# Layer 1's tail: weights of the further tiles fetched by SyncE with register addresses in place of GpSimd's indirect DMAs

## The chip, the core and the metric

The kernel runs as one program on one core of a Trainium2 chip. The metric is the time of one execution on the device, in microseconds (us). A core has five instruction streams that are used here, each strictly in order: TensorE (PE, matmuls and transposes), VectorE (DVE), ScalarE (ACT), GpSimd (POOL) and SyncE (SP). SP does no arithmetic in this kernel: it issues DMAs. POOL does element-wise work and also issues the indirect DMAs, whose row numbers come from a table in SBUF.

## What is computed

Two transformer layers on x of shape (8, 256, 128), all in float32. Each layer is adaptive layer norm, causal attention with 16 heads, a gated residual, a second adaptive layer norm and a mixture of experts. Layer 1's mixture, which is what the change touches, is in essence:

```
p        = sigmoid(h @ gate_w + gate_b)            # 16 experts
v, e     = top_k(p, 2);  v = v / sum(v)            # 2 experts for each token
y[e]     = (silu(h @ wg[e]) * (h @ wu[e])) @ wd[e] # hidden size 64
x        = x + gb * (h + shared_mlp(h) + v0 * y[e0] + v1 * y[e1])
```

Which experts a token takes is known only on the device, so the tokens of an expert have to be collected at run time.

## The kernel before

Tokens are held in four groups of 512 (`NW = 4`). For the first three groups of layer 1, the mixture is done sparsely: `route1` picks the experts, and `place_steps` scatters each token's row (indirect DMAs of POOL, line 916) to the DRAM tensor `xs`, which is sorted by expert. The last group, whose routing is known too late, is done densely at the end (`dense_hidden`, `dense_gate`, `dense_project`).

The sorted rows are worked in 40 tiles of 128 rows, four tiles to a step, so ten steps `m = 0..9` (`NQ = 10`). The tiles of steps 0 to 3 are the first 128 rows of each of the 16 experts: their place and their weights are known beforehand, and the weights lie in SBUF already. The tiles of steps 4 to 9, the further tiles, hold whatever is above 128 rows. Which expert each of these tiles has is worked out by `tables_steps` into two tables: `rowi` (first row in `xs`) and `widx` (first row of the expert's weights, plus the partition).

Each step has these parts, by their functions:

- `fetch_rows1(m)` (lines 1717 to 1726) loads the rows into `xg`. For m of 4 and above these are four DMAs of SP with a register as address (line 1026). The registers are filled beforehand, all 24 of them in one go, by `find_rows1` (line 1017, a register load from `rowi`). `xg` has four buffers.
- `fetch_weights1(m)` (lines 1732 to 1745), only for m of 4 and above, loads four times 128x256 floats (128 KB each) into `wt`. For m = 4 and 5 these are a register load from `widx` (line 1741) and a DMA of SP (line 1745) for each tile. For m = 6 to 9 they are an indirect DMA of POOL for each tile (`load_weights`, line 1030).
- `turn1(m)` transposes the rows on PE (line 1760), copies them out of PSUM on ACT (line 1762), and then issues `fetch_rows1(m + 4)`.
- `hidden1(m)` does the two hidden matmuls (line 1771), the SiLU on ACT (line 1776) and the product on DVE (line 1777).
- `project_tiles(m)` does the output matmuls (line 1784), copies them to `ysb` on DVE (line 1790) and stores them to the DRAM tensor `ys` by a DMA of SP (line 1791). `ysb` has three buffers, so the copy of step m waits until the store of step m - 3 has landed.

After the ten steps, `gather1` fetches each token's two results from `ys` by 24 indirect DMAs of POOL (line 1038). Each of them may need any row of `ys`, so the first waits for the last store. Then follow the combination (`combine1`, lines 1893 to 1899), the last group's dense mixture and the output.

The order on each engine is written out by hand (`manual_schedule`): an engine's instructions stand in the order in which the functions are called. The attention loop calls steps that are hung on its iterations by `at_end(n, ...)`; its last iterations, 29 to 31, take the tables, the weights of steps 4 and 5, the rows of steps 0 to 3 and the 24 register loads. After the loop the steps are called one by one with the tail of the attention, in this order around the change: `turn1(0)`, `turn1(1)`, `hidden1(0)`, `turn1(2)`, `hidden1(1)`, `project_tiles(0)`, `turn1(3)`, `hidden1(2)`, `project_tiles(1)`, `tables()` (the second half, 13 instructions of DVE), `turn1(4)`, `hidden1(3)`, and so on, with parts of the norm and the routing of batches 6 and 7 (`norms`, `go6`) between them. `spread_last` (line 1627, matmuls of the last batch's attention denominators) stands between `project_tiles(8)` and `project_tiles(9)`.

SP's DMAs go round eight completion semaphores, and a DMA waits until the one eight before it has landed.

Of the kernel before, what the change touches and what calls it, by code (L numbers as in the profile page):

```python
# [557 lines left out]
def fast_path(ctx: ExitStack, tc: tile.TileContext, i: dict, out: bass.AP, bad: bass.AP):  # L558
# [496 lines left out]
    def ps_ln(shape, name):  # L1055
        return pp.tile(shape, F32, tag="p", name=name)
# [5 lines left out]
    z1 = Sorted(xp, "1", E1, 3 * TT, ND1)  # L1062
# [298 lines left out]
    def at_end(n, *steps):  # L1361
        ends.setdefault(n, []).extend(steps)
# [291 lines left out]
    def norm1(bs):  # L1654


        kept = []
        name = f"{bs[0]}_{bs[1]}"

        def tokens():  # L1660
            ht = tokens1[bs] = lp.tile([P, 2 * bs[1], P], F32, tag="ht", name=f"ht1_{name}")
            nc.gpsimd.tensor_tensor(by_batch(ht), by_batch(kept[0]), rows_of_span(mdb1[:, CB], bs), ALU.mult)
            nc.gpsimd.tensor_tensor(by_batch(ht), by_batch(ht), rows_of_span(mdb1[:, SB], bs), ALU.add)

        def add_h():
            xn, xs = kept[0], span_tokens(bs)
            nc.gpsimd.tensor_tensor(by_batch(xn), by_batch(tokens1[bs]), rows_of_span(mdb1[:, GB], bs), ALU.mult)
            nc.gpsimd.tensor_tensor(xs, xs, xn, ALU.add)

        return [  # L1670
            *layernorm_parts(
                bs[0] // 2, md[1], SB, CB, f"1b{name}", ps_ln, lambda w, xn: kept.append(xn),
                range(2 * (bs[0] % 2), 2 * (bs[0] % 2 + bs[1])),
            ),
            tokens, add_h,
        ]
# [37 lines left out]
    NQ = (E1 + ND1) // 4  # L1714
    starts = []

    def fetch_rows1(m):

        xg = sq["x", m] = lp.tile([P, 4, P], F32, tag="xg", bufs=4, name=f"xg1_{m}")
        if m < E1 // 4:  # L1720
            nc.sync.dma_start(
                out=xg, in_=z1.xs.rearrange("(e r) c -> r e c", r=z1.cap)[0:P, bass.ts(m, 4), :]
            )
        else:
            for t in range(4):
                z1.load_rows(xg[:, t, :], 4 * m + t - E1, starts.pop(0))

    def find_rows1(m):

        starts.extend(z1.row_start(4 * m + t - E1) for t in range(4))  # L1730

    def fetch_weights1(m):

        tag, n = {4: ("wt", 2), 5: ("wt", 2), 9: ("rb", 1)}.get(m, ("v", 3))
        wt = sq["w", m] = lp.tile([P, 4, WD1], F32, tag=tag, bufs=n, name=f"wt1_{m}")
        for t in range(4):
            d = 4 * m + t - E1
            if m > 5:
                z1.load_weights(wt[:, t, :], i["wpk1"], d)
                continue  # L1740
            r = nc.values_load(
                z1.widx[0:1, d : d + 1], engines=[mybir.EngineType.SP], min_val=0, max_val=(E1 - 1) * P,
                skip_runtime_bounds_check_because="an expert's number, 128 times",
            )
            nc.sync.dma_start(out=wt[:, t, :], in_=i["wpk1"][bass.ds(r, P), :])  # L1745

    def weights1(m, t):

        rows = bass.ts(t % 2, I1)
        if m < E1 // 4:  # L1750
            e = 4 * m + t
            return w1["wg1"][:, bass.ts(e, I1)], w1["wu1"][:, bass.ts(e, I1)], w1["wd1"][rows, e // 2, :]
        wt = sq["w", m]
        return wt[:, t, 0:I1], wt[:, t, I1 : 2 * I1], wt[rows, t, 2 * I1 :]

    def turn1(m):
        xT_ps = ps_ln([P, 4, P], f"xT1_{m}")
        xg = sq.pop(("x", m))
        for t in range(4):
            nc.tensor.transpose(xT_ps[:, t, :], xg[:, t, :], ident)  # L1760
        xT = sq["xT", m] = lp.tile([P, 4, P], F32, tag="xT", name=f"xTs1_{m}")
        nc.scalar.copy(xT, xT_ps)
        if m + 4 < NQ:
            fetch_rows1(m + 4)

    def hidden1(m):
        xT = sq.pop(("xT", m))
        gu = pp.tile([P, 2, 2, P], F32, tag="s", name=f"gu1_{m}")
        for what in range(2):
            for t in range(4):  # L1770
                nc.tensor.matmul(  # L1771
                    out=gu[bass.ts(t % 2, I1), what, t // 2, :], lhsT=weights1(m, t)[what],
                    rhs=xT[:, t, :], start=True, stop=True,
                )
        a = sq["a", m] = lp.tile([P, 2, P], F32, tag="aq", name=f"aq1_{m}")
        nc.scalar.activation(a, gu[:, 0], AF.Silu)
        nc.vector.tensor_tensor(a, a, gu[:, 1], ALU.mult)

    def project_tiles(m):
        a = sq.pop(("a", m))  # L1780
        y = [pp.tile([P, 2, P], F32, tag=tag, bufs=1, name=f"yq1_{m}_{tag}") for tag in ("o", "sum")]
        for t in range(4):
            k = t % 2
            nc.tensor.matmul(
                out=y[k][:, t // 2, :], lhsT=a[bass.ts(k, I1), t // 2, :], rhs=weights1(m, t)[2],
                start=True, stop=True,
            )
        ysb = lp.tile([P, 2, 2, P], F32, tag="ysb", bufs=3, name=f"ysb1_{m}")
        for k in range(2):
            nc.vector.tensor_copy(ysb[:, :, k, :], y[k])  # L1790
        nc.sync.dma_start(
            out=z1.ys[bass.ds(4 * m * P, 4 * P), :].rearrange("(t p) c -> p t c", p=P),
            in_=ysb.rearrange("p a k c -> p (a k) c"),
        )
# [157 lines left out]
    for bs in ((0, 2), (2, 2), (4, 1), (5, 1)):  # L1952
# [14 lines left out]
        if bs[0] < 5:  # L1967
            at_end(n + 7, add)
    tables = one(z1.tables_steps(ps_ln, True))
    at_end(29, tables, lambda: fetch_weights1(4), lambda: fetch_weights1(5))  # L1970
    at_end(30, *[lambda m=m: fetch_rows1(m) for m in range(4)], *[lambda m=m: find_rows1(m) for m in range(4, NQ)])

    for n in range(N):
        b, u = divmod(n, 4)
# [18 lines left out]
            step()  # L1993


    for m in (6, 7):
        fetch_weights1(m)
    norms = [norm1((b, 1)) for b in (B - 2, B - 1)]
    go6, go7 = (one(route1((b, 1))) for b in (B - 2, B - 1))
    values1(*divmod(N - 1, 4))  # L2000
# [1 line left out]
    turn1(0)  # L2002
    turn1(1)
    hidden1(0)
    for m in (8, 9):
        fetch_weights1(m)
    add()
    turn1(2)
    hidden1(1)
    project_tiles(0)  # L2010
    turn1(3)
    hidden1(2)
    project_tiles(1)
    tables()
# [77 lines left out]
def adaln_two_layers(tc: tile.TileContext, i: dict, out: bass.AP):  # L2092
    nc = tc.nc
    with tc.tile_pool(name="flag", bufs=1) as fp:
        bad = fp.tile([1, 1], mybir.dt.int32, name="bad")
        fast_path(tc, i, out, bad)
        redo = nc.values_load(bad[0:1, 0:1], min_val=0, max_val=1, skip_runtime_bounds_check_because="a comparison")
        with tc.If(redo > 0):
            general_path(tc, i, out)
# [84 lines left out]
```

## Time and profile before

| | us |
|---|---|
| median of 14 runs | 640.78 |
| lowest and highest of them | 635.79, 642.7 |
| the profiled execution, its own time | 643.87 |
| the profiled execution, span from first to last instruction | 641.7 |

Busy shares of the span: PE 88%, PE's weight loads 63%, DVE 54%, POOL 48%, ACT 45%. The attention of layer 1 ends at 542.4 us; the ten steps run from 544.9 to 585.7, the 24 gathers from 589.0 to 619.0, and the rest to 641.7.

An instruction's line such as "570.15 0.66 PE L1760 MATMUL xT<-ident,xg ... x4" is: start in us from the span's start, length in us of the merged group, engine, line of the kernel, operation, output<-inputs, and how many were merged. Brackets at its end give the idle time of the engine before it and what ended it. "SPq" is SP's instruction stream. Register loads and the arithmetic of registers are not counted as busy, so gaps between SP's DMAs may be full of them.

### The profile page before, as it was taken

What the parts mean: (1) busy time and instruction counts of PE and PEld (TensorE: products, weight loads), DVE (VectorE), ACT (ScalarE), POOL (GpSimd) and SP (SyncE); (2) the same over time, 40 slices, a digit from 0 to 9 for tenths busy, and PEclk for the clock granted to TensorE, in tenths of its full rate; (3) what the DMA queues carried; (4) which work ended last, traced back from release to release, by engine and by line L of the source; (5) the groups of instructions that cost most, each with busy time, mean ns of one, the idle gap of its engine ahead of it and who ended that gap; (6) DMA issues with size and microseconds to landing.
All of it is one profiled execution on the core that took longest, in us unless ns stands there. A gap on an engine that the chain in (4) does not pass through costs nothing.

```text
span 641.7 us, 12934 instructions
## 1 busy us (share of the span) xinstructions
PE 565.6 (88%) x4903; PEld 402.0 (63%) x4903; DVE 349.6 (54%) x1055; ACT 289.1 (45%) x502; POOL 307.6 (48%) x454
## 2 busy tenths in 40 slices
PE   4789887988869999869999999999999997887973
PEld 3445444445569999756667676766777765665453
DVE  4225758577663222233844566575746566456586
ACT  2567665555505555426553444335435351452230
POOL 6232557576631444136652234761364737712773
PEclk9979998888989999989999999999999999789787
DMA  8999970012033999513030303130203034742441
GB/s 285 343 408 397 389 259 21 13 56 91 26 115 90 323 324 320 185 49 137 26 84 10 67 10 76 38 80 1 67 17 84 19 68 138 220 134 74 110 100 70
DMA packets 51377, 85.45 MB, mean 133 GB/s; under 512 B 6428, under 2 KB 30108, under 8 KB 50156
## 3 DMA queue, kind: packets, MB, share of 16 engines
q1 hardware_dynamic: 42140, 57.67, 28.2%
q0 software_dynamic: 9168, 26.88, 13.7%
q8 instruction: 40, 0.66, 0.4%
q14 instruction: 29, 0.24, 0.1%
HBM read 53.46 MB, written 31.07 MB: 132 GB/s over the span
## 4 chain that ended last, share of the span: by engine, by line
PE 38%; DVE 6%; POOL 4%; issue 3%; ACT 2%; DMA 2%; SPq 1%; POOLq 0%; DVEq 0%; ACTq 0%
PE sc L1564 7%; PE o L1586 6%; PE qp L1533 5%; PE vp L1546 5%; PE kp L1533 4%; POOL yg L1038 4%; PE y L1639 4%; PE sum L1594 3%; PE gu L1771 1%; PE xT L1760 1%; DMA xg<-xs 1%; DVE tc L1894 1%; SPq L1745 1%; PE rp L1627 1%; ACT L751 1%
## 5 line engine op out<-in xcount | busy, mean ns | idle before, releaser
L804 POOL TENSOR_SCALAR_AFFINE_SELECT pt<-pt 128x256 f32<-128x256 f32 (+1 forms) x176 | 89.0, 530 | 136.7 <-ACT pt L1567 80.2
L1038 POOL DMA_INDIRECT yg<-ys,yidx x56 | 53.8, 960 | 54.5 <-issue 34.0
L1030 POOL DMA_INDIRECT wt<-in_wpk_dram,widx x47 | 44.3, 942 | 56.2 <-PE xT L1312 49.9
L1134 ACT ACTIVATE pt<-sc 128x1024 f32<-128x1024 f32 x48 | 46.6, 1021 | 29.8 <-PE sc L1130 25.9
L1567 ACT ACTIVATE pt<-sc 128x768 f32<-128x768 f32 x64 | 48.4, 808 | 25.5 <-PE sc L1564 25.4
L1323 ACT ACTIVATE hst<-hp,wt 128x128 f32<-128x128 f32 x136 | 38.9, 368 | 31.7 <-ACT hst L1323 18.3
L1564 PEld LDWEIGHTS sc<-q,k 64*128 64x128 f32 x512 | 41.5, 187 | 16.4 <-issue 11.4
L1564 PE MATMUL sc<-q,k 64*128 64x256 f32 (+1 forms) x512 | 50.5, 336 | 0.0
L1586 PE MATMUL o<-pt,v 128*64 128x256 f32 (+1 forms) x512 | 48.7, 332 | 1.8 <-POOL pt L804 1.8
L1549 ACT COPY v<-vp 128x512 f32<-128x512 f32 x32 | 18.8, 586 | 67.7 <-PE vp L1546 56.8
L1333 DVE COPY ysb<-yt 128x128 f32<-128x128 f32 x39 | 11.4, 292 | 61.0 <-PE yt L1329 61.0
L1586 PEld LDWEIGHTS o<-pt,v 128*64 128x64 f32 x512 | 31.8, 136 | 19.7 <-POOL pt L804 5.6
L1537 DVE COPY q<-qp 128x512 f32<-128x512 f32 x32 | 22.0, 688 | 38.9 <-PE qp L1533 38.9
L1321 PE MATMUL hp<-xTs,wt 128*128 128x128 f32 x272 | 36.8, 278 | 3.8 <-DMA wt<-in_wpk_dram,widx 2.7
L1533 PE MATMUL qp<-h,wq 128*128 128x256 f32 x128 | 37.0, 412 | 1.3 <-DVE sh L1282 1.3
L916 POOL DMA_INDIRECT xs<-ht0b,idx x32 | 31.5, 983 | 13.0 <-issue 4.6
L1546 PE MATMUL vp<-wv,h 128*128 128x512 f32 x64 | 36.2, 648 | 1.1 <-DVE q L1537 1.1
L1130 PE MATMUL sc<-qm,k 32*128 32x512 f32 x192 | 34.9, 743 | 2.6 <-ACT pt L1134 1.8
L1321 PEld LDWEIGHTS hp<-xTs,wt 128*128 128x128 f32 x272 | 33.0, 191 | 5.9 <-issue 4.4
L1329 PE MATMUL yt<-wt,hst 128*128 128x128 f32 x272 | 35.8, 275 | 0.0
L1533 PE MATMUL kp<-h,wk 128*128 128x256 f32 x128 | 33.8, 388 | 0.0
L1329 PEld LDWEIGHTS yt<-wt,hst 128*128 128x128 f32 x272 | 33.0, 192 | 0.0
(292 smaller groups left out, 1169.0 us busy)
## 6 DMA issues: line engine op xcount, KB each, us to landing
xs<-zero SPq DMA_DIRECT2D x1, 12288.0 KB
xs<-zero SPq DMA_DIRECT2D x1, 8192.0 KB
rb<-rd SPq DMA_DIRECT2D x14, 512.0 KB
mdb<-mrd SPq DMA_DIRECT2D x2, 2048.0 KB
xg<-xs SPq DMA_DIRECT2D x63, 64.0 KB
wst<-in_wpk_dram SPq DMA_DIRECT2D x5, 514.0 KB
ys<-ysb SPq DMA_DIRECT2D x10, 256.0 KB
ys<-ysb SPq DMA_DIRECT2D x39, 64.0 KB
```

Source lines behind the costliest of these rows:

```text
L804: nc.gpsimd.affine_select(out=pt, in_=pt, compare_op=ALU.is_ge, fill=0.0, base=0, pattern=[[0, pt.shape[1]], [1, P]], channel_multiplier=-1,)
L1030: nc.gpsimd.indirect_dma_start(out=wt, out_offset=None, in_=packed, in_offset=bass.IndirectOffsetOnAxis(ap=self.widx[:, d : d + 1], axis=0),)
L1038: nc.gpsimd.indirect_dma_start(out=yg[:, k, :], out_offset=None, in_=self.ys[:, :], in_offset=bass.IndirectOffsetOnAxis(ap=self.yidx[:, j, ...
L1134: nc.scalar.activation(pt[:, bass.ts(half, 2), :], sc, AF.Exp)
L1321: nc.tensor.matmul(out=hp[:, c, :], lhsT=wt[:, bass.ts(c, P)], rhs=xT, start=True, stop=True)
L1323: nc.scalar.activation(hs[:, c, :], hp[:, c, :], AF.Gelu_apprx_tanh, bias=wt[:, WB + c : WB + c + 1])
L1329: nc.tensor.matmul(out=y, lhsT=hs[:, c, :], rhs=wt[:, bass.ds(WF + c * P, P)], start=(c == 0), stop=(c == FC - 1))
L1533: nc.tensor.matmul(out=ps_[:, n, :], lhsT=w1[f"w{what}1"][:, bass.ts(2 * u + n, P)], rhs=hb, start=True, stop=True)
L1546: nc.tensor.matmul(out=vp, lhsT=hb[:, bass.ts(j, P)], rhs=w1["wv1"][:, bass.ts(half, 512)], start=True, stop=True)
L1564: nc.tensor.matmul(out=sc[:, n, cols], lhsT=k[r, m, bass.ts(kb, P)], rhs=q[r, m, qs], start=True, stop=True)
L1567: nc.scalar.activation(pt, sc[:, :, 0:384], AF.Exp, scale=1.0 / math.sqrt(D1))
L1586: nc.tensor.matmul(out=o[bass.ts(n, D1), m, qs], lhsT=v[:, kb, bass.ts(4 * (u % 2) + 2 * m + n, D1)], rhs=pts[m][:, n, cols], start=(kb == ...
```

## The change

The branch to `load_weights` goes: `fetch_weights1` uses SP's register load and register-addressed DMA for all of steps 4 to 9. The calls for steps 6 to 9 move as well. Step 6's is hung on iteration 30 of the attention loop, behind the 24 register loads; step 7's comes after `hidden1(0)`, step 8's after `turn1(2)`, step 9's after `turn1(3)`. On the other engines nothing is added, removed or put in another order but that POOL's 16 indirect DMAs are gone.

```diff
@@ -1735,9 +1735,6 @@
         wt = sq["w", m] = lp.tile([P, 4, WD1], F32, tag=tag, bufs=n, name=f"wt1_{m}")
         for t in range(4):
             d = 4 * m + t - E1
-            if m > 5:
-                z1.load_weights(wt[:, t, :], i["wpk1"], d)
-                continue
             r = nc.values_load(
                 z1.widx[0:1, d : d + 1], engines=[mybir.EngineType.SP], min_val=0, max_val=(E1 - 1) * P,
                 skip_runtime_bounds_check_because="an expert's number, 128 times",
@@ -1968,7 +1965,8 @@
-    at_end(30, *[lambda m=m: fetch_rows1(m) for m in range(4)], *[lambda m=m: find_rows1(m) for m in range(4, NQ)])
+    at_end(30, *[lambda m=m: fetch_rows1(m) for m in range(4)], *[lambda m=m: find_rows1(m) for m in range(4, NQ)],
+           lambda: fetch_weights1(6))
@@ -1993,8 +1991,6 @@
-    for m in (6, 7):
-        fetch_weights1(m)
     norms = [norm1((b, 1)) for b in (B - 2, B - 1)]
@@ -2002,13 +1998,14 @@
     turn1(0)
     turn1(1)
     hidden1(0)
-    for m in (8, 9):
-        fetch_weights1(m)
+    fetch_weights1(7)
     add()
     turn1(2)
+    fetch_weights1(8)
     hidden1(1)
     project_tiles(0)
     turn1(3)
+    fetch_weights1(9)
     hidden1(2)
     project_tiles(1)
     tables()
```

In SP's stream the order from the 24 register loads on becomes: weights 6, rows 4, rows 5, weights 7, rows 6, weights 8, store 0, rows 7, weights 9, store 1, rows 8, store 2, rows 9, stores 3 to 9. Before, it was the same without the weights, and with rows 6 ahead of store 0 as now.

## The prediction

> **What bounds the kernel now.** I read the chain of waits first, over the tail; then the timelines of SP, PE and POOL from 530 to 592 us, the instructions by line for the fetches, and the busy time by stretch for the clock. The chain shows what the tail hangs on:
>
> ```profile
> 570.90 0.59 ACT xTs L1762
> 571.51 1.28 ACT L1691
> 579.43 3.88 PE rp L1627 x16
> 585.66 2.28 DMA ys<-ysb
> 588.95 0.97 POOL yg L1038
> ```
>
> From 588.95 POOL issues 24 gathers, one each 1.25 us, then four element-wise instructions, and the end follows. All of it stands behind the last `ys` store, issued at 585.66. So what delays step 9's store delays the end one for one, and what only makes POOL idle sooner gains nothing. POOL's timeline says the same of the fetches that go away:
>
> ```profile
> 557.59 0.95 POOL L1030 DMA_INDIRECT wt<-in_wpk_dram,widx  x1 [0.30 <-issue]
> 568.27 0.73 POOL L1668 TENSOR_TENSOR x<-x,xn1b 128x256 f32<-128x256 f32 x1
> 588.95 0.97 POOL L1038 DMA_INDIRECT yg<-ys,yidx  x1 [19.94 <-issue]
> ```
>
> The last weight fetch is issued at 557.59, and POOL then stands idle for 19.94 us before the gathers. POOL is free there. SP is not:
>
> ```profile
> 533.99 7.28 SPq L1745 DMA_DIRECT2D wt<-in_wpk_dram  x8
> 541.36 2.05 SPq L1721 DMA_DIRECT2D xg<-xs  x4
> 551.12 6.21 SPq L1026 DMA_DIRECT2D xg<-xs  x12
> 557.43 0.38 SPq L1791 DMA_DIRECT2D ys<-ysb  x1
> 558.06 2.62 SPq L1026 DMA_DIRECT2D xg<-xs  x4
> 560.79 0.42 SPq L1791 DMA_DIRECT2D ys<-ysb  x1
> 561.46 1.90 SPq L1026 DMA_DIRECT2D xg<-xs  x4
> 563.47 0.39 SPq L1791 DMA_DIRECT2D ys<-ysb  x1
> 564.42 1.93 SPq L1026 DMA_DIRECT2D xg<-xs  x4
> ```
>
> The gap between 543.4 and 551.1 is not idle; by the instructions of line 1017 it is the register loads, end to end:
>
> ```profile
> L1017 SPq TENSOR_LOAD <-rowi x24: 261/267/281, 543.5 to 550.6; - x24
> ```
>
> So SP works without a pause from 533.5 to 557.8, and its rows are late already: rows 4 could go at 545.6, when `turn1(0)` has freed the buffer, and go at 551.12. What saves the steps is that PE consumes slower still. The reader should set the last rows beside the transposes that need them:
>
> ```profile
> 570.15 0.66 PE L1760 MATMUL xT<-ident,xg 128*128 128x128 f32 x4
> 572.76 0.66 PE L1760 MATMUL xT<-ident,xg 128*128 128x128 f32 x4
> ```
>
> These are `turn1(8)` and `turn1(9)`. The last DMA of rows 8 is issued at 563.02 and lands at 564.95, of rows 9 at 566.01 and 567.87 (the trace's landings). The slack is 5.2 and 4.9 us. That is all that SP may be delayed.
>
> **What the change removes.** 16 indirect DMAs of POOL, 16 x 1.25 = 20 us of POOL between 538.8 and 558.6. Behind them stand only the two instructions of `add` (L1667, L1668 at 558.56) and the token instructions at 564.25, which waited 3.94 us for DVE. Nobody waits for either, so this is worth 0 on the path; the cover is POOL's idle 19.94 us. A second effect is on the transfers: POOL's 16 x 128 KB fly at the same time as rows 0 to 3, of which DMA 1 takes 4.84 us to land in the chain of waits and the last one 5.9, while the first took 3.5. `turn1(1)` waited 1.24 us for it. If it landed in 2.28, as a store of the same 256 KB does, it would be there at 544.1, and `turn1(1)` could follow `turn1(0)` at 544.5 in place of 546.8: a gain of up to 2.3 us at the head of the steps. I take 0, because SP's stream behind 543.4 does not wait for PE, and SP is what will be late.
>
> **What it adds to SP.** A weight fetch is a register load, register arithmetic and a DMA. The eight of steps 4 and 5 show the price: their DMAs start at 535.19, 536.05, 536.88, 537.72, 538.55, 539.38, 540.20, so 0.83 us each. A row DMA, whose register is ready, takes 0.53 (551.12 to 557.43 for 12). A store takes about 0.5 with its wait. From the end of the register loads at 550.9, and with no wait on PE in between (steps 0 to 3 are transposed by 554), the stream is:
>
> - weights 6 (4 x 0.83 = 3.3) to 554.2, rows 4 (2.1) to 556.4, rows 5 to 558.5
> - weights 7 to 561.8, rows 6 to 564.0, weights 8 to 567.3, store 0 to 567.8, rows 7 to 570.0
> - weights 9 to 573.3, store 1 to 573.8, rows 8 to 576.0, store 2 to 576.5, rows 9 to 578.6
>
> All 16 weight fetches are queued ahead of rows 8: 13.3 us, of which waits that SP had before (it stood for stores at 557.8, 560.5 and 563.4) give back about 0.8. The last DMA of rows 8 starts at 575.5, of rows 9 at 578.1. Alone, a row DMA lands in 1.8 to 2.2 us (551.12 to 552.93; 566.01 to 567.87); I take 2.1. So rows 8 are there at 577.6 and rows 9 at 580.2, against transposes at 570.15 and 572.76: **+7.45 us each**.
>
> A second line is late by as much. `ysb` has three buffers, so DVE's copy of step 5 waits for store 2. Stores take 2.28 to land; store 2 goes at 576.1 and lands at 578.4, where the copy stood at 570.38: +8.0. Behind it on DVE stands the router's add (L1690 at 571.20, then 579.2), but ACT can use that only after its table load, which follows the copy of `turn1(8)` by 0.6 us and takes 1.28: 577.6 + 0.7 + 0.6 + 1.3 = 580.2, against 572.80. So ACT stays at +7.45, and store 2 has about 0.6 us to spare there.
>
> From there the chain is the old one: SiLU tables, steps 7 to 9, `rp`, store 9 (from 570.15 to 585.66, 15.5 us), then the gathers. Nothing in it is hidden, so +7.45 goes to the end. The weights are in time: weights 9 land near 575, `hidden1(9)` comes after 582.
>
> **PE's clock.** Waiting costs PE its clock. The busy time by stretch shows it after the idle times that end at 544.9 and 562.8:
>
> ```profile
> 546.00:553.00 7.00, 6.20 (x44) 4.91 (x46) 0.42 (x1) 3.23 (x6) 5.17 (x7) 0.51 0.70 202
> 563.00:567.00 4.00, 4.00 (x29) 3.24 (x29) 1.72 (x7) 1.52 (x2) 1.45 (x2) 0.57 0.66 173
> 567.00:572.00 5.00, 5.00 (x62) 4.17 (x62) 2.82 (x8) 2.78 (x6) 1.46 (x2) 1.00 0.42 119
> ```
>
> The seventh column is the granted clock. At half clock a hidden step takes 1.9 us (550.84) in place of 1.02 (568.55). In the changed kernel PE waits for rows 4 from about 555 to 558, and for stores 0 and 1 near 568 to 570.5 and 573.5 to 576.5, so half clock is likely up to about 580 to 583. Up to there SP is later than PE, and it costs nothing. On the path it slows `turn1(8)` (+0.4) and perhaps `hidden1(8)`, half hidden by ACT: +0.5 in all. Bounds: 0 if the clock is full by 577, and +3.9 if it is still half during `rp` (3.88 at full clock).
>
> **A rule against the trace.** The register load is 0.267 us in the row above. The Trainium skill (DMA: Bandwidth & Descriptors, "Latency and other measured facts") gives a floor of about 600 ns for it; by that a fetch would take 0.33 more, 16 of them 5.3, and the forecast would be about 654. The row is of the same instruction on the same engine and decides. The same page ("Issuing engines are not separate DMA queues") says that spreading DMAs over several engines saves only issue time on the sequencers, usually small beside the transfer. Here that issue time is the whole matter, and the change puts it all on one sequencer.
>
> **Sum.** 7.45 + 0.5 = +8.0 us. The profiled execution would have a span of 649.7 and, with the 2.2 around it, a time of 651.9; its own time of 643.87 lies 3.1 above the median. From the median, 640.8 + 8.0 = **648.8 us**. What a measurement of this kernel can tell from no change is about 0.3%, 1.9 us.
>
> **The rivals.**
>
> *SP still worse.* Two of the 32 register-addressed DMAs held SP for 1.06 us in place of 0.33 (540.20, 558.59), both while transfers landed slowly, in over 3.5 us. Were four of the 36 weight and row DMAs up to rows 8 held so, +2.9; with `rp` at half clock, +3.9 in place of 0.5. Together 7.45 + 2.9 + 3.9 = +14, or 655; one of them alone 651.7 to 652.2. For it: the bytes in flight do not fall, they only come by another queue. Against: the first five fetches of steps 4 and 5, before POOL's began, landed in 2.0 to 2.1 us.
>
> *SP less late.* If a fetch's register load ran beside the DMA issue ahead of it, a fetch would cost 0.83 - 0.27 = 0.56, 16 of them 4.3 less, and rows 8 would be late by 7.45 - 4.3 = 3.1 us: 644.4 with the clock's 0.5. Against: seven fetches in a row show 0.83.
>
> *Faster, by the transfers.* Rows 0 to 3 land sooner without POOL's traffic, and the steps start 2.3 us earlier, all of it kept: 640.8 - 2.3 = 638.5. This decides only if SP is not late, that is if a fetch adds under 5.2 / 16 = 0.33 us to SP's stream. The rows of line 1745 say 0.83.
>
> *No effect.* If the weights moved but SP had idle room that I misread, the end stays. The end-to-end register loads speak against it.
>
> **How the numbers follow.** Chances: the forecast (+6.5 to +9.5) 0.68, worse SP (+9.5 to +14) 0.15, less late (+2.5 to +6.5) 0.10, faster 0.05, no effect 0.02. So faster 0.05, same 0.02, slower 0.93. The range leaves out the two sides beyond +3.7 and +12.7: 644.5 to 653.5.
>
> **What would show it.** Right: SP's timeline without a gap from 550.9 to about 578, weight DMAs 0.83 apart; rows 9 issued near 578 instead of 566; PE idle before L1760 with the releaser "DMA xg<-xs" in the later steps and DVE's L1790 idle on stores; the first gather near 597; POOL's gathers still 1.25 apart. Wrong: `turn1(8)` waiting for DVE or ACT and not for rows; weight DMAs much closer or further apart than 0.83; a shift of the first gather that does not reach the end.

## The result, and the profile after

The changed kernel takes 649.17 us (median of 10 runs, 646.72 to 652.23), the kernel before 640.70 (47 runs). The ratio is 1.0147, with a 95% interval of 1.0123 to 1.0172: **slower by 7.9 to 11.0 us**, in the middle 9.4 (the two medians lie 8.5 apart). Forecast were 648.8 and +8.0.

One thing has to be known to read the numbers below. The result and the last experiment ran on chips where the kernel before takes 641 us; the other experiments ran on three chips where it takes 670 to 672. In the experiments each ratio is against runs of the kernel before on the same chip; the kernel before was profiled only where it takes 641. The distance from the first row DMA of step 0 to the last store of `ys` hardly depends on the chip for a kernel in which POOL issues no DMA in that stretch (54.6 us in the changed kernel on the one, 54.2 on the other), so it is used to compare SP's work.

SP's timeline of the changed kernel (L1742 weights, L1026 rows, L1788 stores):

```profile
546.15 2.87 SPq L1742 DMA_DIRECT2D wt<-in_wpk_dram  x4
549.27 4.02 SPq L1026 DMA_DIRECT2D xg<-xs  x8
553.87 3.77 SPq L1742 DMA_DIRECT2D wt<-in_wpk_dram  x4
557.89 1.93 SPq L1026 DMA_DIRECT2D xg<-xs  x4
560.72 2.84 SPq L1742 DMA_DIRECT2D wt<-in_wpk_dram  x4
563.66 0.38 SPq L1788 DMA_DIRECT2D ys<-ysb  x1
564.29 1.89 SPq L1026 DMA_DIRECT2D xg<-xs  x4
566.68 2.83 SPq L1742 DMA_DIRECT2D wt<-in_wpk_dram  x4
569.61 0.38 SPq L1788 DMA_DIRECT2D ys<-ysb  x1
570.23 1.89 SPq L1026 DMA_DIRECT2D xg<-xs  x4
572.23 0.38 SPq L1788 DMA_DIRECT2D ys<-ysb  x1
572.85 1.89 SPq L1026 DMA_DIRECT2D xg<-xs  x4
```

Four weight fetches stand ahead of rows 4, 6, 7 and 8 each. Store 0 goes at 563.66, though DVE had its tile ready at 546.2: it stood in the stream behind them. The chain of waits of the same kernel then runs through a store and not through a row load:

```profile
566.68 0.33 SPq L1742
568.34 0.33 SPq L1742
569.61 2.62 DMA ys<-ysb
572.32 0.44 DVE ysb L1787
572.80 0.58 PE yq_o L1781
574.35 1.04 PE xT L1757 x4
...
590.65 2.27 DMA ys<-ysb
593.13 0.74 issue
593.86 1.00 POOL yg L1038
```

Read upwards from 574.35, which is `turn1(8)`: PE was held by the output matmuls of step 5 (L1781), these by DVE's copy of step 4 (L1787), that by store 1, and store 1 by the weights of step 9. PE, DVE and POOL say what they waited for, in the brackets of their timelines:

```profile
551.24 1.39 PE L1757 MATMUL xT<-ident,xg 128*128 128x128 f32 x3 [3.65 <-DMA xg<-xs]
...
566.38 0.42 DVE L1787 COPY ysb<-yq_o 128x256 f32<-128x256 f32 x1 [5.29 <-DMA ys<-ysb]
...
572.32 0.43 DVE L1787 COPY ysb<-yq_o 128x256 f32<-128x256 f32 x1 [4.34 <-DMA ys<-ysb]
...
593.86 1.00 POOL L1038 DMA_INDIRECT yg<-ys,yidx  x1 [29.08 <-DMA ys<-ysb]
```

POOL now idles 29.08 us ahead of the gathers, where it idled 19.94. Distances from the first row DMA of step 0 (541.36 before, 536.06 after), in us:

| | before | after | difference |
|---|---|---|---|
| `turn1(1)` | 5.43 | 4.01 | -1.42 |
| last DMA of rows 8 | 21.65 | 35.73 | +14.08 |
| `turn1(8)` | 28.79 | 38.22 | +9.43 |
| last store | 44.30 | 54.60 | +10.30 |
| end of the span | 100.35 | 110.94 | +10.59 |

The two profiled executions differ by only 643.87 to 649.15 = 5.28, because the part ahead of the first row DMA, nearly the same code in both, was 5.30 shorter in the second. That part differs as much between profiles of one kernel (541.56 and 537.57 in the two of the constant addresses below), so the tail alone shows the change.

### The profile page after: what moved, and what is told of

The parts are those of the page before. It is cut to its first block, busy times and chain, and to the rows that moved or that the text cites. A ratio compares the mean times of both kernels' runs of the same rounds, so it can differ in the third digit from the quotient of the medians.

```text
span 647.0 us, 12977 instructions
## 1 busy us (share of the span) xinstructions
PE 566.6 (88%) x4903; PEld 405.9 (63%) x4903; DVE 350.0 (54%) x1055; ACT 289.0 (45%) x502; POOL 291.9 (45%) x438
## 4 chain that ended last, share of the span: by engine, by line
PE 38%; DVE 5%; SPq 4%; POOL 4%; issue 3%; DMA 1%; ACT 1%; POOLq 0%; DVEq 0%; ACTq 0%
PE sc L1564 7%; PE o L1586 6%; PE qp L1533 5%; PE vp L1546 5%; PE kp L1533 4%; POOL yg L1038 4%; PE y L1639 4%; PE sum L1594 3%; SPq L1742 1%; PE gu L1768 1%; SPq L1017 1%; SPq L1738 1%; DMA ys<-ysb 1%; DVE tc L1891 1%; SPq L1026 1%
## 5 line engine op out<-in xcount | busy, mean ns | idle before, releaser
L1030 POOL DMA_INDIRECT wt<-in_wpk_dram,widx x31 | 29.1, 939 | 51.3 <-PE xT L1312 49.7
L1321 PE MATMUL hp<-xTs,wt 128*128 128x128 f32 x272 | 36.6, 278 | 2.0 <-DMA wt<-in_wpk_dram,widx 0.8
L1130 PE MATMUL sc<-qm,k 32*128 32x512 f32 x192 | 33.1, 710 | 3.6 <-ACT pt L1134 2.8
```

The source lines that it names most:

```text
L1130: nc.tensor.matmul(out=sc[:, n, :].rearrange("p (a q) -> p a q", q=rhs.shape[2]), lhsT=k[r, cols], rhs=rhs, start=True, stop=True,)
L1321: nc.tensor.matmul(out=hp[:, c, :], lhsT=wt[:, bass.ts(c, P)], rhs=xT, start=True, stop=True)
```

## The experiments

Theory A: the loss is SP's time for issuing 16 more fetches ahead of the rows and stores. Rival B: the loss is the bytes, now in flight at another time or by another queue.

### The issue time without the bytes

The kernel before, with POOL's fetches kept, and on SP at the places of the change 16 register loads and DMAs of 256 bytes:

```diff
+    junk = lp.tile([1, 16, I1], F32, bufs=1, name="junk")
+    def spend1(m):
+        for t in range(4):
+            d = 4 * m + t - E1
+            r = nc.values_load(z1.widx[0:1, d : d + 1], engines=[mybir.EngineType.SP], ...
+            nc.sync.dma_start(out=junk[:, 4 * (m - 6) + t, :], in_=i["wpk1"][bass.ds(r, 1), 0:I1])
```

> The kernel before, with POOL still fetching all weights of steps 6 to 9, and with 16 register loads and register-addressed DMAs of SP added at the places in SP's stream where the changed kernel has its fetches, but each DMA moves 256 bytes into a spare buffer. Theory A (SP's issue time is what costs): if such a DMA costs SP the same 0.83 us, the tail is as late as in the changed kernel, +8 to +10 us, 649 to 651; if a DMA of one row is cheaper to issue, 16 times the measured cost, less the slack of 5 us and the 0.8 of old waits: at 0.55 us a fetch +3, 644. Rival B (the bytes on SP's queue, that is the transfers, cost): within 1 us of before, since no bytes to speak of are added. Shown by the distance of the new DMAs in SP's timeline and by the start of the ninth transpose (turn1(8)) against the fetch of rows 0.

Measured: 679.95 against 671.74, ratio 1.0132 (1.0089 to 1.0176), +8.9 us. In SP's timeline of this kernel, four such fetches of 256 bytes (L1738) take 3.23:

```profile
566.43 3.23 SPq L1738 DMA_DIRECT2D junk<-in_wpk_dram  x4
569.91 3.02 SPq L1026 DMA_DIRECT2D xg<-xs  x4
573.98 3.40 SPq L1738 DMA_DIRECT2D junk<-in_wpk_dram  x4
577.47 0.40 SPq L1803 DMA_DIRECT2D ys<-ysb  x1
```

The fetches start 0.99 us apart, no closer than the 128 KB fetches of the changed kernel (0.82 to 0.87). The issue of the DMA itself takes 0.28 in place of 0.33; the register load ahead of it (L1734) takes mostly 0.48 here in place of 0.27, which was not explained. The chain of waits has the same links as in the changed kernel, from the fetches through store 1 and DVE's copy to `turn1(8)`:

```profile
583.10 0.49 SPq L1734
584.13 2.44 DMA ys<-ysb
586.66 0.43 DVE ysb L1802
587.14 0.58 PE yq_o L1796
588.69 1.04 PE xT L1772 x4
```

The same kernel on a second such chip:

> The kernel of e1 again, with the same theories: A says that 16 loads and DMAs of 256 bytes delay the rows by what they take of SP (0.83 us each if the issue does not depend on the size: +8 to +10 us where the kernel before takes about 641; at 0.55 each +3); B says within 1 us of before.

Measured: 677.60 against 670.98, ratio 1.0106 (1.006 to 1.0152), +7.1 us, the fetches again 1.0 apart. What follows: nearly no bytes, and a loss of the size of the change's 9.4 (6.0 to 11.8 and 4.0 to 10.2 by the intervals). A stands. As a size it is rough, since a fetch is dearer here and SP was slowed at the head on this kind of chip, as shown further down. B is not needed; it isn't excluded that bytes add something.

### A shorter fetch: constant addresses

The changed kernel with the 16 fetches at addresses that are known beforehand, so without register load and arithmetic (these steps then multiply with the weights of other experts):

```diff
+            if m > 5:
+                nc.sync.dma_start(out=wt[:, t, :], in_=i["wpk1"][bass.ts(d % E1, P), :])
+                continue
```

> The changed kernel, with the 16 fetches of steps 6 to 9 at constant addresses: no register load and no register arithmetic, the same bytes by the same queue at the same places. (It computes with the wrong experts' weights.) Theory A: a fetch costs SP about 0.38 us (the issue of 0.33 and a gap), 16 of them 6.1, less 0.8 and the slack of 5: +0 to +1.5 us, 640.7 to 642.2. Rival B (bytes): as slow as the changed kernel, 649 to 650.

Measured: 663.76 against 671.74, ratio 0.988 (0.9852 to 0.9908). On a second chip:

> The kernel of e2 again: the same bytes by SP's queue as in the changed kernel, at constant addresses. A says +0 to +3 us against a kernel before of about 641 (its trace of the first job had the last store 47.0 us behind the fetch of rows 0, against 44.3 before and 54.6 changed); B says as slow as the changed kernel in the same job.

Measured: 660.93 against 670.98, ratio 0.9858 (0.981 to 0.9906). SP's timeline of the first of the two:

```profile
562.27 1.80 SPq L1739 DMA_DIRECT2D wt<-in_wpk_dram  x4
564.17 0.38 SPq L1791 DMA_DIRECT2D ys<-ysb  x1
564.79 1.91 SPq L1026 DMA_DIRECT2D xg<-xs  x4
566.75 1.84 SPq L1739 DMA_DIRECT2D wt<-in_wpk_dram  x4
```

A fetch takes 0.47 here (562.27 to 564.17 for four) in place of 0.83, and the same bytes go by the same queue. 16 x 0.36 = 5.8 less is what A asks for. The last store lies 47.04 and 48.49 behind the first row DMA, against 54.15 in the changed kernel on such a chip: 7.1 and 5.7 less. A sizes it, B gives 0. Of the 5.7, 3.6 are in the medians of the same chip (660.93 against the 664.57 of the next section).

### The changed kernel on a second kind of chip

That these kernels beat 671 was odd, as they are still some 3 to 4 us later at the last store than the kernel before in its profile. So the changed kernel itself was run there:

> The changed kernel itself, beside the experiments, since in the job of the first four the kernel before took 671.7 us, 31 more than in the job of the prediction's result. Theory A: where the kernel before takes about 641, this takes 8 to 11 more. Where the kernel before takes about 672, its tail is held up by something that the first job does not show, in stretches in which all engines crawl; e2 to e4, which take fetches from POOL, were faster than before there by 5 to 13 us, so this could be within 5 us of before on either side.

Measured: 664.57 against 670.98, ratio 0.9882 (0.9844 to 0.992): **faster by 5.4 to 10.5 us there** (the medians are 6.4 apart), with the same lateness at the last store (54.15). Something else costs the kernel before more on such a chip. Fewer and more fetches by POOL show where. Step 6 alone by SP, then steps 6 and 7, then none and those of steps 4 and 5 by POOL as well:

```diff
-            if m > 5:
+            if m not in (4, 5, 6):        # the second kernel: (4, 5, 6, 7); the third: ()
                 z1.load_weights(wt[:, t, :], i["wpk1"], d)
                 continue
```

> Only step 6's weights by SP, at the changed kernel's place; steps 7 to 9 by POOL as before. Theory A: SP is later by 3.3 us, under the slack of 5.2 of rows 8: no change, 639.7 to 641.7, and rows 8 land before their transpose. Rival C (each fetch costs the end its share): a quarter of the loss, +2.4 us, 643.1.

> Steps 6 and 7 by SP, steps 8 and 9 by POOL. Theory A: SP later by 6.7 us, less 0.6 of old waits and the slack of 5.2: about +1 us, 641 to 643. Rival C: half of the loss, +4.7 us, 645.4.

> The opposite of the change: the weights of steps 4 and 5 too by POOL's indirect DMAs, behind the attention's last mask. SP then has no weight fetch at all, and rows 0 to 3 go out when the last scatter has landed (2.8 us sooner than before: 538.6 in place of 541.4). Theory A (SP's stream sets the start of the steps): 2 to 3 us faster than before. Rival D (the steps are set by PE and DVE, and SP's fetches at their head are hidden as well): no change, within 1 us. Rival B (the bytes beside rows 0 to 3): slower, since now all of POOL's fetches fly beside them, +1 to +3.

Measured, with POOL's fetches in brackets: 666.36 (12), ratio 0.9915 (0.989 to 0.994); 658.98 (8), ratio 0.9815 (0.9791 to 0.9839); 683.02 (24) against 670.98, ratio 1.0153 (1.0108 to 1.0198). None of the three is what A had said, no change, about +1 and 2 to 3 less: those sums were for a chip of 641. What orders the four times, with the kernel before, is how many fetches POOL issues: 683, 671, 666 and 659 us at 24, 16, 12 and 8, so 5 to 7 us for each four (with none, in the changed kernel, SP's lateness outweighs the gain). The timelines of the kernel with 12, POOL's last fetches first, then DVE, then ACT:

```profile
550.29 0.95 POOL L1030 DMA_INDIRECT wt<-in_wpk_dram,widx  x1 [0.30 <-issue]
551.54 0.94 POOL L1030 DMA_INDIRECT wt<-in_wpk_dram,widx  x1 [0.30 <-issue]
552.50 0.73 POOL L1667 TENSOR_TENSOR xn1b<-ht,mdb 128x256 f32<-128x256 f32 x1
```

```profile
542.07 0.69 DVE L1598 COPY ou<-o 128x512 f32<-128x512 f32 x1 [2.09 <-PE sum L1594]
554.95 1.76 DVE L1602 RECIPROCAL r<-sum 128x256 f32<-128x256 f32 x1 [12.19 <-remote]
```

```profile
555.00 1.07 ACT L1762 COPY xTs<-xT 128x512 f32<-128x512 f32 x2 [22.78 <-remote]
```

POOL issues its train at 1.25 each and is not slowed. DVE starts nothing from 542.8 to 554.95, 2.5 us after the train's end, though by PE's timeline the matmuls ahead of its reciprocal ended at 541.3. ACT copies the transposes of `turn1(0)` at 555.00, which PE had done at 545.1; the kernel before in its profile (on the other kind of chip) makes that copy at 545.60, in the middle of POOL's train. ACT's idle time ahead of it is 22.78 us here, 26.95 with 24 fetches by POOL and 12.32 in that profile. The releaser "remote" or "issue" names nothing on this core. PE did its two transposes meanwhile and then waited 9.28 for ACT. SP is slowed too: its 24 register loads end 14.56 us behind the first row DMA, in place of 9.5. So on these chips DVE, ACT and SP are held while POOL issues indirect DMAs back to back; by what, these runs do not show. It happens again in the 24 gathers: from the first gather to the end the changed kernel takes 71.6 us there and 53.1 on the other.

### No fetches at all

The changed kernel with the fetches of steps 6 to 9 left out (these steps multiply with weights of other experts, which lie in SBUF):

```diff
-        if m < E1 // 4:
-            e = 4 * m + t
+        if m < E1 // 4 or m > 5:
+            e = (4 * m + t) % E1
-           lambda: fetch_weights1(6))
...
-    fetch_weights1(7)
...
-    fetch_weights1(8)
...
-    fetch_weights1(9)
```

> The changed kernel with the weight fetches of steps 6 to 9 left out: neither POOL nor SP fetches them, and these steps multiply with weights that lie in SBUF already (so their results are of the wrong experts). SP's stream is that of the kernel before, POOL has nothing to issue before the gathers. Theory A (SP's issue time is the whole loss of the changed kernel, and POOL's fetches are worth nothing on the path): the last store lies 42 to 44.5 us behind the first row DMA of step 0, as in the kernel before (44.3) or up to 2.3 less, against 54 to 55 in the changed kernel. Rival B (the weights' bytes, by whatever queue, hold the rows): clearly under 42. Where the kernel before takes about 671 us, this one takes 10 to 15 us less if the hold of the other engines comes from POOL issuing indirect DMAs back to back, and 0 to 3 less if it does not; where it takes 641 us, 0 to 2.5 less.

Measured: 654.09 against 670.38, ratio 0.9742 (0.9694 to 0.9789), by the medians 16.3 less. The last store lies 41.57 behind the first row DMA: 12.6 less than with SP's fetches, and 2.7 less than in the kernel before. A's lower end (42) was missed by 0.4, on the side that rival B had named. The 2.7 is the head's gain that the prediction bounded at 2.3: `turn1(2)` comes at +5.56 in place of +8.36, and with SP on time it is kept to the end. That it comes from the transfers beside rows 0 to 3 was not tested by itself. From the first gather on it still takes 69.0 us, by ACT's timeline with long stops between its instructions:

```profile
588.63 1.28 ACT L1691 ACT_TABLE_LOAD   x1
595.56 0.23 ACT L1691 ACTIVATE p<-p 128x32 f32<-128x32 f32 x1 [5.64 <-issue]
...
619.34 1.09 ACT L1827 ACTIVATE a<-gud 128x512 f32<-128x512 f32 x2 [12.83 <-remote]
```

POOL issues the 24 gathers from 585.45 to 615.2; the instruction at 619.34 had stood 12.83 us and comes only after them. With 16 us for this, the numbers of such a chip add up: without fetches 640.7 - 2.7 + 16 = 654.0 (measured 654.1), changed 649.2 + 16 = 665.2 (664.6). The kernel before is 640.7 + 16 + 14 = 671 if POOL's train of 16 weights costs 14; that last figure is only what is left over.

### The weights by ACT, and later on SP

Two attempts to keep the fetches away from POOL and from the rows. Weights 4, 5, 6 by ACT behind the attention loop, 7 by SP after `turn1(3)`, 8 and 9 after `turn1(5)`:

```diff
+            act = m in (4, 5, 6)
-            nc.sync.dma_start(out=wt[:, t, :], in_=i["wpk1"][bass.ds(r, P), :])
+            (nc.scalar if act else nc.sync).dma_start(out=wt[:, t, :], in_=i["wpk1"][bass.ds(r, P), :])
```

> No weight fetch by POOL, and SP's share made small: weights of steps 4, 5, 6 are fetched by ACT (register load and DMA on ACT, right behind the attention loop, where ACT is idle), those of step 7 by SP after turn1(3), those of 8 and 9 by SP after turn1(5), behind the rows of step 9. Theory A (SP's issue time ahead of the rows is the loss): 4 of the 16 fetches of the changed kernel stay ahead of rows 8 (4 x 0.83 = 3.3 us, within the slack of 5.2), the 8 of steps 4 and 5 no longer stand ahead of rows 0; the last store lies 43 to 47 us behind the first row DMA of step 0, that DMA goes up to 3 us sooner, and the kernel takes 0 to 3 us less than the kernel before where that takes 641, and 12 to 16 less where it takes 671. Rival B (the bytes in flight): the same bytes in the same stretch, so 50 us or more and no gain over the changed kernel.

Measured: 663.50 against 670.38, ratio 0.9901 (0.9874 to 0.9928), so 4.8 to 8.4 less and not A's 12 to 16; the last store at +51.46, not 43 to 47. B's number came out (50 or more, and next to no gain over the changed kernel's 664.57); its cause is looked at below. The other left all 16 on SP, weights 6 after `turn1(3)`, 7 after `turn1(4)`, 8 and 9 after `turn1(5)`:

> The changed kernel with the same 16 fetches on SP, only placed later: weights 6 after turn1(3), 7 after turn1(4), 8 and 9 after turn1(5), so that 8 of them stand ahead of rows 9 and none ahead of rows 7, and the last 8 behind all rows. Theory A: rows 8 are late by 4 x 0.83 = 3.3 us, within their slack of 5.2, rows 9 by 6.6 against 4.9, but stores 1 and 2 and the last weights are pushed too; the last store lies 46 to 50 us behind the first row DMA of step 0, against 54 to 55 in the changed kernel. Rival B (the bytes of the weights, not SP's stream): 53 to 55, since the same bytes come by the same queue. Where the kernel before takes about 671 us: 8 to 11 less than it by A, about 6 less by B; where it takes 641: 2 to 6 more by A.

Measured: 669.66 against 670.38, ratio 0.9997 (0.9968 to 1.0025); the last store at +53.95, where A had said 46 to 50. In time both were off: A had 8 to 11 less, B about 6 less. (Its median lies 5 us above the changed kernel's on another such chip, at the same distance to the last store; the profiled execution, 666.43, is the shortest of ten. That difference is not explained.) B had the distance again, but not the cause: `turn1(8)` comes at +27.63, earlier than in the kernel before, with the same bytes on the same queue. SP's and DVE's timelines of this kernel show what I had left out:

```profile
568.48 1.93 SPq L1026 DMA_DIRECT2D xg<-xs  x4
570.98 6.24 SPq L1742 DMA_DIRECT2D wt<-in_wpk_dram  x8
577.32 15.12 SPq L1788 DMA_DIRECT2D ys<-ysb  x7
```

```profile
579.99 0.42 DVE L1787 COPY ysb<-yq_o 128x256 f32<-128x256 f32 x1 [6.04 <-DMA ys<-ysb]
```

The eight fetches behind rows 9 are ahead of store 3, which goes at 577.32 (+39.2, in the kernel before +25.1). DVE's copy of step 6 waits 6.04 for it. The rows up to 8 were freed and the stores held. In the kernel with ACT it is the same eight and the same store (573.82, +36.6), and one more thing at the head:

```profile
532.62 14.98 ACTq L1744 DMA_DIRECT2D wt<-in_wpk_dram  x12
547.64 1.07 ACT L1761 COPY xTs<-xT 128x512 f32<-128x512 f32 x2 [15.93 <-DMA wt<-in_wpk_dram]
```

ACT needed 15 us for its 12 fetches (0.86 apart, with a stop before the fifth, which by the chain of waits goes at 541.22, when SP's first row DMA has landed; the two share a completion semaphore), and its copy of `turn1(0)`, which could go at 541.9, went at 547.64.

### The same fetch on POOL

The kernel before, with POOL's 16 indirect DMAs replaced by register loads and register-addressed DMAs of POOL, at the same places:

```diff
-            if m > 5:
-                z1.load_weights(wt[:, t, :], i["wpk1"], d)
-                continue
+            pool = m > 5
-                z1.widx[0:1, d : d + 1], engines=[mybir.EngineType.SP], min_val=0, max_val=(E1 - 1) * P,
+                z1.widx[0:1, d : d + 1], engines=[mybir.EngineType.Pool if pool else mybir.EngineType.SP],
-            nc.sync.dma_start(out=wt[:, t, :], in_=i["wpk1"][bass.ds(r, P), :])
+            (nc.gpsimd if pool else nc.sync).dma_start(out=wt[:, t, :], in_=i["wpk1"][bass.ds(r, P), :])
```

> The kernel before with one edit: POOL still fetches the weights of steps 6 to 9, at the same places, but each by a register load of POOL and a DMA with a register address in place of the indirect DMA. SP's stream stays that of the kernel before. Theory A (the loss of the changed kernel is SP's issue time, so the fetches may stay with POOL in any form): the last store lies 41 to 45 us behind the first row DMA of step 0, against 44.3 before and 54 to 55 in the changed kernel. Where the kernel before takes about 671 us there is a second question, what holds the other engines while POOL issues: if it is the indirect form, this kernel takes 10 to 16 us less (as the one without fetches, 16 less); if it is POOL's issuing of DMAs or the bytes, within 3 us of the kernel before. Where the kernel before takes 641: 0 to 3 less. Rival B (the bytes in flight on any queue delay the rows): no better than the kernel before in the distance to the last store.

Measured: 639.61 against 641.32, ratio 0.9983 (0.9957 to 1.0009), on a chip like that of the result. The last store lies at +44.43, against +44.30 before and +54.60 with the change. POOL's timeline:

```profile
545.83 0.54 POOL L1744 DMA_DIRECT2D wt<-in_wpk_dram  x1 [0.81 <-DMA xg<-xs]
546.76 0.54 POOL L1744 DMA_DIRECT2D wt<-in_wpk_dram  x1 [0.40 <-issue]
```

A register-addressed fetch takes POOL 0.93 (the first five 0.53 to 0.61), an indirect one 1.25, and the last goes 10.2 us behind the first row DMA in place of 16.2. Nobody waited for POOL, so the time is the same. This is the cleanest of the comparisons: the same instructions for the same bytes, on POOL's stream at no cost, on SP's at 9.4 us. It separates the stream from the form of the address and from the bytes, and the loss goes with the stream, as A has it. Whether this form also frees the other engines on the second kind of chip was not seen, as this ran on the first. For the same reason no version is shown to beat both kernels on both kinds.

## Why the prediction was right

The mechanism, SP's issue time, was right and the time came out. That 648.8 lies within 0.4 of the median is in part luck: by the profiles the tail lost 10.6 us and not 8.0, and it is the two medians, 8.5 apart, that make it look closer.

- **SP is the bound.** Right. From the register loads to rows 9 SP works almost without a gap, the weights 0.82 to 0.87 apart but for the one DMA of the next point. The fetches of 256 bytes and the constant addresses show that it is issue time.
- **Rows 8 late.** The last DMA of rows 8 was to start 34.1 behind the first row DMA (575.5 - 541.36); it did at 35.73, so the stream was mis-sized by 1.6. One weight DMA held SP for 1.296 in place of 0.33 (554.70): +0.96. A wait of 0.36 ahead of weights 8 was not counted; some 0.3 is spread over the rest. The landing took 2.10, as assumed. Holds were priced in the rival "SP still worse", with four of 36; there was one. In the changed kernel's second profile it is the same DMA again (1.342), so it is hardly chance.
- **The second line.** The prediction gave store 2 and the copy of step 5 "about 0.6 us to spare" and did not ask the same of store 1, behind which PE's output matmuls of step 5 stand, ahead of `turn1(8)`. It was store 1 and the copy of step 4 that came last, 0.4 after rows 8 (which landed at 573.89, against `turn1(8)` at 574.28). So `turn1(8)` waited by way of DVE and not for rows, one of the prediction's own signs of being wrong; the cost was 0.4, since both lines hang on the same weights in SP's stream. 7.45 + 1.6 + 0.4 = 9.45, which is the +9.43 of the table.
- **The clock.** +0.5 was said from `turn1(8)` on; from there to the last store it took 16.38 in place of 15.51, +0.87. About half of it, 0.45, lies ahead of `rp`: `turn1(8)` took 1.04 in place of 0.60 at half clock. The rest lies from the start of `rp` on, which stood 0.36 for DVE between its halves; the sum had no term for that. By the busy time by stretch the granted clock was 0.50 from 567 to 580 and 0.95 from 580 to 586, so `rp` was at about full clock, as taken.
- **Nothing hidden behind it.** Right: 10.30 late at the last store, 10.59 at the end.
- **The head's gain taken as 0.** Right for this kernel: `turn1(1)` came 1.4 sooner and `turn1(4)` 0.9 later. The gain is real, 2.7 without any fetch, and is lost as soon as SP is late.
- **POOL's 20 us worth 0.** Right on chips like that of the result, as far as the runs go: a train of POOL that ends 6 us sooner moved nothing there, and the sum with 0 came out. Wrong on the second kind, where other engines stand during the train; there its removal pays for SP's lateness and some 6 to 8 us more. The profile of before could not show this, since on its chip ACT and PE run through the train.
- **A page against the trace.** The Trainium skill (DMA: Bandwidth & Descriptors, "Issuing engines are not separate DMA queues") says that spreading DMAs over engines saves only sequencer time, usually small beside the DMA itself. That it is sequencer time agrees with 256 bytes costing as much as 128 KB. That it is small does not hold here: a fetch takes 0.83 us of SP, and 13 of the 16 land 2.0 to 2.3 us after their issue. Sixteen such times in one stream are 13.3 us, and 9.4 of them show in the result.

## What to carry to other kernels

Before DMAs are moved to another engine's queue, add up that queue's issue time up to each transfer somebody waits for, at the duration its own rows show (here 0.83 us for a fetch with register load), and set it against the slack of that transfer; here the bytes could be left out of the sum. Count the stores in the same stream too: late stores hold buffers, and moving the fetches from ahead of the loads to ahead of the stores gained nothing. Here a stream with idle time, POOL's, took the same fetches for nothing.

## What was not expected of the hardware

- Two kinds of chips: the kernel before takes 641 us on some and 670 to 672 on three others (each used once, so it could also be a state of the chip). On the latter DVE stood 12.19 us, with its input ready since 541.3, while POOL issued indirect DMAs back to back, and the part from the gathers on took 68.6 to 72.0 us in all eleven profiles, against 52.7 to 53.1 in the three on the other kind. What holds them was not found; the releasers name nothing on the core.
- A change can be 1.5% slower on the one kind and 1.2% faster on the other, by two effects, SP's issue time and the hold during POOL's train; only the first was followed to its cause.
- A fetch's price by its form, per DMA: 0.47 us at a constant address on SP, 0.83 with a register load on SP, 0.86 on ACT, 0.93 on POOL (0.53 to 0.61 for its first five), 1.25 as an indirect DMA of POOL.
